# Two images side by side in a fixed order in one layer, overlapping phases in the next: one change to a four-layer kernel

## The chip, the cores and the metric

The kernel runs on one core of a Trainium2 chip. The core has five engines that work side by side, each with its own in-order queue: TensorE (PE, matrix products into PSUM), VectorE (DVE, element-wise work), ScalarE (ACT, functions by table), GpSimd (POOL), and SyncE (SP), which issues most DMA transfers. The metric is the device time of one execution in microseconds (us). All data is float32.

## The reference

The input is `x`, four images of 128 channels and 64 x 64 pixels. Four layers follow each other:

- Layer 0: self-attention over the 4096 pixels of each image.
- Layer 1: two quantized 3 x 3 convolutions, each followed by an "adder" convolution (a sum of absolute differences) with batch norm, and a residual.
- Layer 2: per image `x = x + attention(norm(x))`, then `x = x + mlp(norm(x))`.
- Layer 3: illumination and gradient maps split the image, then a selective scan along the 4096 pixels.

The change touches layer 2 and the preparation ahead of layer 3's scan. Layer 2 in the reference, cut:

```python
def _biasfree_ln(x, w):              # over the 128 channels of a pixel
    mu = jnp.mean(x, axis=1, keepdims=True)
    var = jnp.mean((x - mu) ** 2, axis=1, keepdims=True)
    return x / jnp.sqrt(var + EPS) * w[None, :, None, None]
...
    x1, x2 = (x[:, :C2], x[:, C2:])                       # 64 + 64 channels
    x1 = _gelu(_conv(x1, dw_w, dw_b, groups=C2, pad=1))   # depthwise 3 x 3
    x2 = _gelu(_conv(x2, qkvl_w, qkvl_b))                 # q, k, v, lfeat, 32 channels each
...
    qk = jnp.einsum('bcn,bdn->bcd', qf, kf)               # of pooled q and k, 32 x 32
...
    return jnp.concatenate([x1, lfeat, out], axis=1)
...
    h = _gelu(_conv(x, fc1_w, fc1_b))                     # 128 -> 512 channels
    h = h + _gelu(_conv(h, pos_w, pos_b, groups=h.shape[1], pad=1))
    return _conv(h, fc2_w, fc2_b)                         # 512 -> 128
```

Layer 3 before its scan: a sigmoid gate and a product with the gradient map (the "split" into a low part and the part `fh`), an RMS norm of `fh` over channels, a projection to 2 x 256 channels, a causal convolution with 4 taps and Silu on the first 256 (`xs`), Silu on the others (`sz`), a projection of `xs` to 40 values per pixel, and from 8 of these `delta = softplus(...)` for 256 channels and `du = delta * xs`.

## The kernel before, in words

The kernel is written with tiles and pools: a program in Python issues instructions, each engine executes its own in a planned order, and semaphores are derived from the tiles that are read and written. A pool gives out buffers in turn, and a tile waits until the one that had its buffer is done with. Where an instruction goes through `keep_in_program_order`, its place in its engine's queue is that of the program text; without it a planner may move it forward or back.

An image lies as 128 partitions (channels) by 4096 columns (pixels); a block is 8 rows of the image, 512 columns, one PSUM bank; an image has 8 blocks. `inner(xp, b, k)` is block `k` of image `b` in the residual stream.

Layer 2 (L603 on) goes through the four images one by one.

- `layernorm` (L634) takes block after block: PE averages over channels (L639), DVE subtracts (L641), ACT squares (L642), PE averages (L644), ACT makes the reciprocal root by Ln and Exp (L82, L83), DVE scales (L647).
- The first norm goes to `hp`, an image with a border of zeros. The first 64 channels go through the depthwise convolution on DVE, nine taps of 64 x 4096 (L670, L672) into `x1`, with Gelu on ACT (L673). The other 64 go through PE and Gelu to `x2` (L660, L663). DVE pools q and k (L678 to L685), PE makes the 32 x 32 product (L690 to L696), ACT its Exp. DVE adds `x1` and a part of `x2` to the stream (L711, L712) and, per block, the attention's result (L715, L719).
- The second norm goes to `m`. Then, in two halves of 32 image rows, four groups of 128 hidden channels each: five products with Gelu into `ht` (L740, L743); a depthwise convolution, for group 0 on PE with diagonal matrices (nine products per block, L753, Gelu L760), for groups 1 to 3 on DVE (nine taps of 128 x 2048, L766 and L768, Gelu L771); the sum with `ht` (L772); and the product back to 128 channels, summed over the groups in four PSUM banks (L776). At the end of a half DVE adds the sums to the stream (L781).
- Buffers: four PSUM banks are shared by all small products, four hold the sums; `ht` and `g` have two buffers each.

`layer3_prepare` (L814 on) takes for each image: the split (L857 to L867: a load `mr` of two map rows, two products into `pm`, Sigmoid on ACT, one product into `pg`, two DVE products, and a store to `low_d`), the norm (L874 to L879), for each of two channel halves the projection into `pre` (L888, L889), the causal convolution with four taps of 128 x 4096 (L891, L893) and Silu (L896), stored to `xs_d`; then the gate Silu (L903, L905) to `sz_d`; then four steps `k2` of 1024 columns: products and copies to `xd` (L916, L919), and for both channel halves the softplus `dv` (L929 to L942: product, bias, Abs, Exp, two DVE operations, Ln, two DVE operations) and on POOL `du` (L945), both stored. Six PSUM banks are shared. `ln_and_exp` (L78) loads ACT's table for Ln and Exp ahead of use.

Neither function pins its order, apart from that table load. What is issued next on an engine is the planner's choice among the instructions of the program text.

Of the kernel before, what the change touches and what calls it, by code (L numbers as in the profile page):

```python
# [1 line left out]

# [6 lines left out]
F32 = mybir.dt.float32  # L9
# [7 lines left out]
P = 128  # L17
B = 4
# [36 lines left out]
def col(ap):  # L55

    return ap.rearrange("(p o) -> p o", o=1)
# [28 lines left out]
def inner(x, b, k):  # L86

    return x[b][:, RB * k : RB * (k + 1), :]
# [513 lines left out]

def layer2(tc, cm, xp, ln1, ln2, dw_w, dw_b, qkvl_w, qkvl_b, fc1_w, fc1_b, pos_w, pos_b, fc2_w, fc2_b):  # L603
    nc = tc.nc
    NCH = 4
    with ExitStack() as ctx:
# [3 lines left out]
        ps = ctx.enter_context(tc.tile_pool(name="l2p", bufs=4, space=PSUM))  # L610
# [8 lines left out]
        ln2_sb = load([1], col(ln2), "ln2")  # L619
        dww = load([TAPS], dw_w, "dww")  # L620
        dwb = load([1], col(dw_b), "dwb")
        qw = load([P], qkvl_w, "qw", P // 2)
# [11 lines left out]
        def layernorm(b, w, out, tag):  # L634
            cm.ln_and_exp(tc)
            for k in range(NB):
                src = inner(xp, b, k)
                pm = ps.tile([P, BK], F32, tag="mm", name=f"pm{tag}{b}_{k}")
                nc.tensor.matmul(pm, cm.mean, src, start=True, stop=True)  # L639
                xc = sb.tile([P, BK], F32, tag="xc", name=f"xc{tag}{b}_{k}")  # L640
                nc.vector.tensor_tensor(rows(xc), src, rows(pm), ALU.subtract)  # L641
                nc.scalar.activation(xc, xc, AF.Square)  # L642
                pv = ps.tile([P, BK], F32, tag="mm", name=f"pv{tag}{b}_{k}")
                nc.tensor.matmul(pv, cm.mean, xc, start=True, stop=True)  # L644
                rs = sb.tile([P, BK], F32, tag="rs", name=f"rs{tag}{b}_{k}")
                cm.rstd(nc, rs, pv)
                nc.vector.scalar_tensor_tensor(out(k), src, w, rows(rs), ALU.mult, ALU.mult)  # L647

        for b in range(B):
            x_all = xp[b]  # L650
            hp = big.tile([P, HP, HP], F32, tag="hp", name=f"hp{b}")
            nc.gpsimd.memset(hp[:, 0:HP:HP - 1, :], 0.0)
            nc.gpsimd.memset(hp[:, 1 : HP - 1, 0:HP:HP - 1], 0.0)
            layernorm(b, ln1_sb, lambda k: hp[:, 1 + RB * k : 1 + RB * (k + 1), 1 : 1 + W], "a")
# [3 lines left out]
            for k in range(NB):  # L658
                pq = ps.tile([P, BK], F32, tag="mm", name=f"pq{b}_{k}")
                nc.tensor.matmul(  # L660
                    pq, qw[64:, :], hp[64:, 1 + RB * k : 1 + RB * (k + 1), 1 : 1 + W], start=True, stop=True
                )
                nc.scalar.activation(x2[:, RB * k : RB * (k + 1), :], rows(pq), AF.Gelu, bias=qb)  # L663

            x1 = big.tile([64, H, W], F32, tag="x1", name=f"x1_{b}")
            for t in range(TAPS):
                y, x = divmod(t, 3)
                v = hp[0:64, y : y + H, x : x + W]
                if t == 0:
                    nc.vector.tensor_scalar(x1, v, dww[0:64, 0:1], None, ALU.mult)  # L670
                else:
                    nc.vector.scalar_tensor_tensor(x1, v, dww[0:64, t : t + 1], x1, ALU.mult, ALU.add)  # L672
            nc.scalar.activation(x1, x1, AF.Gelu, bias=dwb[0:64])  # L673


            cs = big.tile([64, H, W // 2], F32, tag="cs", name=f"cs{b}")
            q, kk = slice(0, 32), slice(32, 64)
            nc.vector.tensor_tensor(cs[q], x2[q, :, 0:W:2], x2[q, :, 1:W:2], ALU.add)  # L678
            nc.vector.tensor_tensor(cs[q, :, 1:], cs[q, :, 1:], x2[q, :, 1 : W - 1 : 2], ALU.add)
            nc.vector.tensor_tensor(cs[kk], x2[kk, :, 0:W:2], x2[kk, :, 1:W:2], ALU.max)  # L680
            pf = big.tile([64, H // 2, W // 2], F32, tag="pf", name=f"pf{b}")
            nc.vector.tensor_tensor(pf[q], cs[q, 0:H:2, :], cs[q, 1:H:2, :], ALU.add)
            nc.vector.tensor_tensor(pf[q, 1:, :], pf[q, 1:, :], cs[q, 1 : H - 1 : 2, :], ALU.add)
            nc.vector.tensor_scalar(pf[q], pf[q], 1.0 / 9.0, None, ALU.mult)
            nc.vector.tensor_tensor(pf[kk], cs[kk, 0:H:2, :], cs[kk, 1:H:2, :], ALU.max)  # L685

            pff = pf.rearrange("p a c -> p (a c)")
            pt = ps.tile([P, 8, 64], F32, tag="mm", name=f"pt{b}")
            for j in range(8):
                nc.tensor.transpose(pt[:, j, :], pff[:, bass.ts(j, P)], cm.ident[0:64, 0:64])  # L690
            qkt = sb.tile([P, 8, 64], F32, tag="qkt", name=f"qkt{b}")
            nc.vector.tensor_copy(qkt, pt)
            pqk = ps.tile([P, 32], F32, tag="mm", name=f"pqk{b}")
            d = slice(96, 128)
            for j in range(8):
                nc.tensor.matmul(  # L696
                    pqk[d, :], qkt[:, j, 32:64], qkt[:, j, 0:32], start=(j == 0), stop=(j == 7)
                )
            mx = sb.tile([P, 2], F32, tag="mx", name=f"mx{b}")
            nc.vector.tensor_reduce(mx[d, 0:1], pqk[d, :], AX.X, ALU.max, negate=True)  # L700
            ex = sb.tile([P, 32], F32, tag="ex", name=f"ex{b}")
            cm.ln_and_exp(tc)
            nc.scalar.activation(ex[d, :], pqk[d, :], AF.Exp, bias=mx[d, 0:1])
            nc.vector.tensor_reduce(mx[d, 1:2], ex[d, :], AX.X, ALU.add)
            ri = sb.tile([P, 1], F32, tag="ri", name=f"ri{b}")
            nc.vector.reciprocal(ri[d], mx[d, 1:2])
            nc.vector.tensor_scalar(ex[d, :], ex[d, :], ri[d], None, ALU.mult)
            st = sb.tile([P, 32], F32, tag="st", name=f"st{b}")
            nc.vector.transpose(st[d, :], ex[d, :])

            nc.vector.tensor_tensor(x_all[0:64], x_all[0:64], x1, ALU.add)  # L711
            nc.vector.tensor_tensor(x_all[64:96], x_all[64:96], x2[64:96], ALU.add)  # L712
            for k in range(NB):
                po = ps.tile([P, BK], F32, tag="mm", name=f"po{b}_{k}")
                nc.tensor.matmul(  # L715
                    po[d, :], st[d, :], x2[d, RB * k : RB * (k + 1), :], start=True, stop=True
                )
                o = inner(xp, b, k)[d]
                nc.vector.tensor_tensor(o, o, rows(po[d, :]), ALU.add)  # L719

            m = big.tile([P, H, W], F32, tag="m", name=f"m{b}")
            layernorm(b, ln2_sb, lambda k: m[:, RB * k : RB * (k + 1), :], "b")

            for half in range(2):
                r0 = half * H // 2
                pf2 = [
                    ps_f.tile([P, BK], F32, tag=f"f{s}", name=f"pf2_{b}_{half}_{s}") for s in range(4)
                ]
                for c in range(NCH):
                    u = f"{b}_{half}_{c}"  # L730

                    ht = sb.tile([P, H // 2 + 2, HP], F32, tag="ht", name=f"ht{u}")
                    nc.gpsimd.memset(ht[:, :, 0:HP:HP - 1], 0.0)
                    edge = 0 if half == 0 else H // 2 + 1
                    nc.gpsimd.memset(ht[:, edge, 1 : 1 + W], 0.0)
                    lo = 1 - half
                    for n in (7, 7, 7, 6, 6):
                        ph = ps.tile([P, BK], F32, tag="mm", name=f"ph{u}_{lo}")
                        src = m[:, r0 - 1 + lo : r0 - 1 + lo + n, :]
                        nc.tensor.matmul(  # L740
                            ph[:, : n * W], f1w[:, bass.ts(c, P)], src, start=True, stop=True
                        )
                        nc.scalar.activation(  # L743
                            ht[:, lo : lo + n, 1 : 1 + W], rows(ph[:, : n * W]), AF.Gelu, bias=f1b[:, c : c + 1]
                        )
                        lo += n
                    g = sb.tile([P, HL], F32, tag="g", name=f"g{u}")
                    if c == 0:
                        for s in range(4):
                            pd = ps.tile([P, BK], F32, tag="mm", name=f"pd{u}_{s}")  # L750
                            for t in range(TAPS):
                                y, x = divmod(t, 3)
                                nc.tensor.matmul(  # L753
                                    pd,
                                    diag[:, t, :],
                                    ht[:, RB * s + y : RB * (s + 1) + y, x : x + W],
                                    start=(t == 0),
                                    stop=(t == TAPS - 1),
                                )
                            nc.scalar.activation(g[:, bass.ts(s, BK)], pd, AF.Gelu, bias=pwb[:, c : c + 1])  # L760
# [688 lines left out]
```

## Time and profile before

| | |
|---|---|
| time before, median of 3 runs | 21609.14 us (21584.60 to 21627.24) |
| the profiled execution | 21531.99 us, span 21530.1 us |
| mean granted clock of PE | 0.959 of full speed |
| PE busy | 19660.2 us, 91% |
| DVE busy | 19088.4 us, 89% |
| ACT busy | 17648.1 us, 82% |
| POOL busy | 7450.4 us, 35% |
| layers 0 and 1, with the residual | 0 to 16816 us |
| layer 2 | 16816 to 18152 us |
| layer 3's preparation | 18152 to about 18890 us |
| layer 3's scan | from there to 21530 us |

The profile is of one execution. Busy time is that in which an engine executed something; it is taken from the records of the trace, times are in us from the first instruction. The slices of the span give the busy share of an engine in each of 40 equal parts, in tenths (9 is 90% or more). A row of a group has a source line, engine, operation, output and inputs with their shapes and the count; after the bar the busy time in all and the mean of one in ns; after the second bar the idle time of the engine before them and what ended it. A row of the waits has the engine and its line, what it waited for, the total, how often and the longest. The profiled execution is 0.36% shorter than the median of the runs.

### The profile page before, as it was taken

What the parts mean: (1) busy time and instruction counts of PE and PEld (TensorE: products, weight loads), DVE (VectorE), ACT (ScalarE), POOL (GpSimd) and SP (SyncE); (2) the same over time, 40 slices, a digit from 0 to 9 for tenths busy, and PEclk for the clock granted to TensorE, in tenths of its full rate; (3) what the DMA queues carried; (4) which work ended last, traced back from release to release, by engine and by line L of the source; (5) the groups of instructions that cost most, each with busy time, mean ns of one, the idle gap of its engine ahead of it and who ended that gap; (6) DMA issues with size and microseconds to landing.
All of it is one profiled execution on the core that took longest, in us unless ns stands there. A gap on an engine that the chain in (4) does not pass through costs nothing.

```text
span 21530.1 us, 322927 instructions
## 1 busy us (share of the span) xinstructions
PE 19660.2 (91%) x139180; PEld 6301.1 (29%) x139180; DVE 19088.4 (89%) x12244; ACT 17648.1 (82%) x9117; POOL 7450.4 (35%) x3822
## 2 busy tenths in 40 slices
PE   9998999999999999999999999999999566779998
PEld 4443222222222222222222222222222122223333
DVE  7886999999999999979999999999999666589998
ACT  5665999999999999979999999999999323566666
POOL 5664222222222222222222222222222000189998
PEclk9999999999999999999999999999999777699999
DMA  0001777777777777767777777777777100289997
GB/s 13 13 5 27 151 153 148 152 154 152 152 152 152 150 149 152 154 132 149 149 149 150 149 148 151 147 149 152 149 154 155 52 0 25 108 230 249 252 253 218
DMA packets 573934, 2959.26 MB, mean 137 GB/s; under 512 B 163981, under 2 KB 164885, under 8 KB 240213
## 3 DMA queue, kind: packets, MB, share of 16 engines
q0 software_dynamic: 294912, 2147.61, 49.8%
q1 hardware_dynamic: 277012, 782.60, 12.8%
q8 instruction: 1089, 17.84, 0.3%
q10 hardware_dynamic: 576, 8.39, 0.1%
q14 instruction: 345, 2.82, 0.0%
HBM read 662.02 MB, written 128.78 MB: 37 GB/s over the span
## 4 chain that ended last, share of the span: by engine, by line
PE 45%; issue 15%; DVE 14%; DMA 13%; ACT 11%; POOL 3%; SPq 0%; POOLq 0%; DVEq 0%; ACTq 0%
PE a1pa L424 16%; PE a2pa L424 13%; ACT aa L455 9%; DMA ma<-ma 9%; PE pe L163 4%; PE pav L206 4%; DVE h L1098 3%; DVE ma L478 3%; DVE da L469 2%; DMA du<-du_d 2%; DVE g L768 1%; PE pd L753 1%; PE mg L1113 1%; POOL dbu L1077 1%; POOL ma L480 1%
## 5 line engine op out<-in xcount | busy, mean ns | idle before, releaser
L480 POOL DMA_DIRECT2D ma<-ma x2048 | 3695.5, 1817 | 10893.4 <-DVE ma L478 7653.1
L455 ACT ACTIVATE aa<-a1pb,a1wn 128x4096 f32<-128x4096 f32 x1920 | 6959.8, 3712 | 412.7 <-PE a1pa L424 269.1
L455 ACT ACTIVATE aa<-a2pb,a2wn 128x4096 f32<-128x4096 f32 x1920 | 6963.3, 3712 | 335.1 <-PE a2pa L424 316.2
L424 PE MATMUL a2pa<-aa,a2pick 128*32 128x512 f32 x30720 | 3624.8, 601 | 82.9 <-ACT aa L455 81.6
L424 PE MATMUL a1pa<-aa,a1pick 128*32 128x512 f32 x30720 | 3608.5, 599 | 84.2 <-ACT aa L455 81.9
L469 DVE TENSOR_SCALAR da<-a2pb,a2wa 128x4096 f32<-128x4096 f32 x1408 | 3269.3, 2348 | 295.7 <-PE a2pa L424 295.5
L469 DVE TENSOR_SCALAR da<-a1pb,a1wa 128x4096 f32<-128x4096 f32 x1408 | 3267.7, 2348 | 252.2 <-PE a1pa L424 252.0
L424 PE MATMUL a1pa<-da,a1pick 128*32 128x512 f32 x22528 | 2684.1, 594 | 15.9 <-DVE da L469 15.9
L424 PE MATMUL a2pa<-da,a2pick 128*32 128x512 f32 x22528 | 2678.4, 593 | 17.9 <-DVE da L469 17.9
L478 DVE TENSOR_SCALAR ma<-a2pb,a2wa 128x2048 f32<-128x2048 f32 x2048 | 2528.9, 1280 | 61.8 <-DMA ma<-ma 61.8
L478 DVE TENSOR_SCALAR ma<-a1pb,a1wa 128x2048 f32<-128x2048 f32 x2048 | 2527.9, 1280 | 58.8 <-DMA ma<-ma 58.7
L1113 PE MATMUL mg<-h,ident 128*128 128x512 f32 x4096 | 1953.2, 614 | 209.4 <-ACT m L1122 173.2
L1098 DVE TENSOR_TENSOR_SCAN h<-da,h,dbu 128x1024 f32<-128x1024 f32 x768 | 1804.2, 2349 | 132.7 <-ACT da L1084 42.2
L424 PEld LDWEIGHTS a2pa<-aa,a2pick 128*32 128x32 f32 x30720 | 984.6, 112 | 2498.3 <-issue 2136.7
L424 PEld LDWEIGHTS a1pa<-aa,a1pick 128*32 128x32 f32 x30720 | 980.8, 111 | 2481.8 <-issue 2121.0
L424 PE MATMUL a2pa<-ma,a2pick 128*32 128x512 f32 x8192 | 1096.5, 608 | 235.0 <-DMA ma<-ma 234.7
L200 POOL TENSOR_TENSOR ssum<-ssum,et 128x512 f32<-128x512 f32 x960 | 1228.7, 1280 | 233.4 <-ACT et L195 166.5
L424 PE MATMUL a1pa<-ma,a1pick 128*32 128x512 f32 x8192 | 1092.4, 606 | 190.6 <-DMA ma<-ma 190.4
L424 PEld LDWEIGHTS a1pa<-da,a1pick 128*32 128x32 f32 x22528 | 715.1, 110 | 1739.3 <-issue 1604.5
L424 PEld LDWEIGHTS a2pa<-da,a2pick 128*32 128x32 f32 x22528 | 713.6, 110 | 1737.2 <-issue 1581.4
L461 DVE SCALAR_TENSOR_TENSOR aa<-a2pb,a2wa,aa 128x4096 f32<-128x4096 f32 x256 | 1147.1, 4481 | 80.3 <-ACT aa L455 80.1
L461 DVE SCALAR_TENSOR_TENSOR aa<-a1pb,a1wa,aa 128x4096 f32<-128x4096 f32 x256 | 1147.0, 4481 | 74.9 <-ACT aa L455 74.8
(294 smaller groups left out, 17912.2 us busy)
## 6 DMA issues: line engine op xcount, KB each, us to landing
ma<-ma POOLq DMA_DIRECT2D x2048, 1024.0 KB, 8.8
dl<-delta_d SPq DMA_DIRECT2D x256, 512.0 KB
dl<-delta_d SPq DMA_DIRECT2D x512, 256.0 KB
du<-du_d SPq DMA_DIRECT2D x256, 512.0 KB
du<-du_d SPq DMA_DIRECT2D x512, 256.0 KB
xs_d<-xs SPq DMA_DIRECT2D x8, 2048.0 KB
sz_d<-sz SPq DMA_DIRECT2D x64, 256.0 KB
delta_d<-dv SPq DMA_DIRECT2D x32, 512.0 KB
```

The lines of the kernel that those rows point to most:

```text
L163: nc.tensor.matmul(pe, k[:, bass.ts(j, P)], unit[u, "q"], start=True, stop=True)
L200: nc.gpsimd.tensor_tensor(unit[u, "sum"], unit[u, "sum"], at, ALU.add)
L206: nc.tensor.matmul(unit[u, "av"], image[u // NB][2][:, j, :], at, start=(j == 0), stop=(j == NJ - 1))
L424: then(nc.tensor.matmul(pa[k][32 * g : 32 * g + 32, :], pick[v][:, 31 - jj : 63 - jj], d[:, bass.ts(4 * at + g, BK)], start=(n // 32, k) n ...
L455: then(nc.scalar.activation(rows(at), view(n, t), AF.Abs, bias=bias, scale=scale))
L461: then(nc.vector.scalar_tensor_tensor(rows(at), view(n, ADDED_TAP), weight(n, ADDED_TAP), rows(at), ALU.max, ALU.add))
L469: then(nc.vector.tensor_scalar(rows(dt), view(n, t), weight(n, t), None, ALU.max))
L478: then(nc.vector.tensor_scalar(rows(mt), v, weight(n, t), None, ALU.max))
L480: then(nc.gpsimd.dma_start(ms[1], ms[0], accum_op=ALU.add))
L753: nc.tensor.matmul(pd, diag[:, t, :], ht[:, RB * s + y : RB * (s + 1) + y, x : x + W], start=(t == 0), stop=(t == TAPS - 1),)
L1098: then(nc.vector.tensor_tensor_scan(t[:, cols][:, s], da[:, s], st[n, "dbu", h][:, cols][:, s], 0.0 if e % 4 == 0 else st["last"], ALU.mul ...
L1113: then(nc.tensor.matmul(pm, cm.ident, st[n, way, h][:, bass.ts(k, BK)], start=(way == 0), stop=(way == 1)))
```

## The change

In layer 2, `first_norm`, `second_norm`, `attention` and `feed_forward` become generators that yield after each step, and a driver steps through two of them in a written order; all their compute instructions go through `keep_in_program_order` (`then`).

- `layernorm` issues in step `s` the mean, subtract and square of block `s`, the second mean, Ln and Exp of block `s - 1`, and the scaling of block `s - 2`.
- The first depthwise convolution reads `hx`, which holds the upper and the lower half of `hp`'s first 64 channels on 128 partitions, brought there by two transfers on SP's queue; a tap is now 128 x 2048.
- The two additions to the stream become transfers from SBUF to SBUF that add (`accum_op`), issued by POOL.
- PSUM: three banks for the small products, one for the attention, four for the sums. `ht` and `g` have three buffers.
- The order: `second_norm(b)` and `first_norm(b + 1)` go beside the last group's taps of image `b - 1`, one tap per two steps; `attention(b + 1)` goes beside `feed_forward(b)`, one step per two. Inside `feed_forward` the products for the next group (`up`) and the dense group of PE (`on_tensor`, three products per step) are issued between DVE's taps (`convolution`).

In layer 3's preparation, `split`, `norm`, `project` and `steps_of` are functions in the same manner. `split(b + 1)` is issued after `project(b)`, and `norm(b + 1)` beside `steps_of(b)`, one step per two. `pre` and the causal convolution go in halves of 2048 columns, the gate in between. The softplus goes in three stages over successive units, with three buffers for `dv`, `ee` and `uu`; `du` is written over `uu`. Eight PSUM banks are shared; `mr` has two buffers in place of three.

```diff
+def together(main, beside, ratio):
+    due = 0.0
+    for _ in main:
+        due += ratio
+        while due >= 1.0:
+            due -= 1.0
+            next(beside, None)
...
-        ps = ctx.enter_context(tc.tile_pool(name="l2p", bufs=4, space=PSUM))
+        ps = ctx.enter_context(tc.tile_pool(name="l2p", bufs=3, space=PSUM))
+        ps_a = ctx.enter_context(tc.tile_pool(name="l2a", bufs=1, space=PSUM))
...
+            hx = big.tile([P, H2 + 2, HP], F32, tag="hx", name=f"hx{b}")
+            for h in range(2):
+                nc.sync.dma_start(hx[64 * h : 64 * h + 64], hp[0:64, H2 * h : H2 * h + H2 + 2, :])
...
-                v = hp[0:64, y : y + H, x : x + W]
+                v = hx[:, y : y + H2, x : x + W]
...
-            nc.vector.tensor_tensor(x_all[0:64], x_all[0:64], x1, ALU.add)
-            nc.vector.tensor_tensor(x_all[64:96], x_all[64:96], x2[64:96], ALU.add)
...
+                then(nc.gpsimd.dma_start(x_all[64:96, half, :], x2[64:96, half, :], accum_op=ALU.add))
...
+                if k == TAPS - 6:
+                    then(nc.scalar.activation(x1, x1, AF.Gelu, bias=dwb))
+                    for h in range(2):
+                        then(nc.gpsimd.dma_start(
+                            x_all[0:64, H2 * h : H2 * h + H2, :], x1[64 * h : 64 * h + 64], accum_op=ALU.add
+                        ))
...
+            yield from up(0, 1)
             for half in range(2):
...
+                after = {0: lambda: gelu(0, 3), 2: lambda: down(0, 3)} if half else {}
+                yield from convolution(half, 1, chain(up(half, 0), up(half, 2)), 1.2, after)
...
+                dense = on_tensor(half)
+                after = {0: lambda: gelu(half, 1), 2: lambda: down(half, 1)}
+                if not half:
+                    yield from convolution(0, 2, chain(islice(dense, 6), up(0, 3)), 1.25, after)
+                    after = {0: lambda: gelu(0, 2), 2: lambda: down(0, 2), 5: lambda: down(0, 0)}
+                    yield from convolution(0, 3, chain(dense, up(1, 1)), 1.25, after)
+                else:
+                    yield from convolution(1, 2, chain(islice(dense, 6), up(1, 3), dense), 1.9, after)
+            gelu(1, 2)
+            yield "last"
+            yield from convolution(1, 3, iter(()), 0, {})
+            yield "rest"
+            down(1, 2)
+            gelu(1, 3)
...
+            tail = until(ended, "rest")
+            together(norms(), tail, 0.5)
+            for _ in tail:
+                pass
+            rest, ended = ended, feed_forward(b)
+            beside = attention(b + 1) if b < B - 1 else iter(())
+            together(chain(rest, until(ended, "last")), beside, 0.5)
+            for _ in beside:
+                pass
...
-        ps = ctx.enter_context(tc.tile_pool(name="l3p", bufs=6, space=PSUM))
+        ps = ctx.enter_context(tc.tile_pool(name="l3p", bufs=8, space=PSUM))
...
-                mr = sb.tile([1, 2, BK], F32, tag="mr", bufs=3, name=f"mr{u}")
+                mr = sb.tile([1, 2, BK], F32, tag="mr", name=f"mr{u}")
...
+        for b in range(B):
+            project(b)
+            if b < B - 1:
+                for _ in split(b + 1):
+                    pass
+            cm.ln_and_exp(tc)
+            beside = norm(b + 1) if b < B - 1 else iter(())
+            for i, _ in enumerate(steps_of(b)):
+                if i % 2:
+                    next(beside, None)
+            for _ in beside:
+                pass
```

## The prediction

> **What bounds the kernel now.** I read the slices of the span first, because the change touches only one stretch of it, then busy time by stage, then the waits inside each stage, and last the duration of one instruction of each group.
>
> ```profile
> PE   9998999999999999999999999999999566779998
> DVE  7886999999999999979999999999999666589998
> PEclk9999999999999999999999999999999777699999
> ```
>
> Nearly all of the span has TensorE (PE) and VectorE (DVE) at nine tenths. Slices 31 to 35 do not: this is layer 2 and the preparation of layer 3. There no engine is full, and TensorE's granted clock is lower. The stages, cut at the first and last instruction of each (columns: length, busy time of PE, its weight loads, DVE, ACT, POOL with counts, then granted clock, DMA share and GB/s):
>
> ```profile
> core 0: us, PE busy (x) PEld busy (x) DVE busy (x) ACT busy (x) POOL busy (x), PEclk, DMA share, GB/s
> 16816.00:18152.00 1336.00, 758.39 (x1626) 309.52 (x1626) 910.86 (x543) 373.99 (x489) 8.81 (x66) 0.77 0.00 1
> 18152.00:18887.00 735.00, 521.71 (x768) 162.24 (x768) 429.61 (x383) 352.34 (x421) 79.22 (x31) 0.67 0.27 105
> 16816.00:16921.00 105.00, 40.81 (x83) 13.11 (x84) 75.69 (x55) 28.95 (x38) 0.48 (x2) 0.61 0.02 6
> 17127.00:17459.00 332.00, 189.53 (x408) 77.36 (x408) 228.32 (x136) 96.61 (x126) 2.44 (x18) 0.77 0.00 0
> 16951.00:16990.00 39.00, 38.52 (x94) 17.38 (x93) 3.04 (x2) 10.71 (x17) 0.24 (x2) 1.00 0.00 0
> 18160.00:18200.00 40.00, 40.00 (x43) 11.66 (x42) 10.68 (x16) 7.35 (x10) 0.00 (x0) 0.50 0.13 47
> ```
>
> Layer 2 takes 1336 us, of which DVE works 911; one steady image takes 332, with DVE 228 and PE 190 in turns. At 16951 PE does dense convolution alone at clock 1.00 while DVE has 3 us of work: a phase where one engine waits for the other. What is waited for (engine, line, releaser, total us, times, longest), layer 2 then layer 3's preparation:
>
> ```profile
> PE pf L776 <- DVE g L772: 242.4, 17, 25.4
> ACT g L771 <- DVE g L768: 211.2, 17, 23.2
> DVE g L772 <- ACT g L760: 200.3, 8, 33.8
> DVE xcb L641 <- PE pmb L639: 73.0, 32, 4.5
> ```
> ```profile
> ACT uu L940 <- DVE ee L939: 108.8, 28, 9.3
> DVE fh L867 <- PE pg L866: 82.2, 29, 5.0
> DVE xd L919 <- PE pxd L916: 65.3, 20, 7.9
> DVE xs L891 <- ACT pre L889: 56.7, 8, 10.0
> ```
>
> DVE is what works most, and it loses 200 us eight times over to PE's dense channel group, and most of the rest to the two norms, one block at a time. The group rows that price the change:
>
> ```profile
> L768 DVE SCALAR_TENSOR_TENSOR g<-ht,pww,g 128x2048 f32<-128x2048 f32 x192 | 444.9, 2348 | 2.9
> L672 DVE SCALAR_TENSOR_TENSOR x<-hp,dww,x 64x4096 f32<-64x4096 f32 x32 | 143.1, 4471 | 0.4
> L711 DVE TENSOR_TENSOR x<-x,x 64x4096 f32<-64x4096 f32 x4 | 17.7, 4417 | 0.1
> L753 PE MATMUL pd<-ht,diag 128*128 128x512 f32 x576 | 249.2, 592 | 0.0
> ```
> ```profile
> L893 DVE SCALAR_TENSOR_TENSOR xs<-pre,cw,xs 128x4096 f32<-128x4096 f32 x24 | 107.6, 4484 | 0.9
> L860 PE MATMUL pm<-mr,iwr 1*128 1x512 f32 x64 | 65.6, 1126 | 0.0
> ```
>
> **Layer 2, DVE work.** The first depthwise convolution goes from 64x4096 to 128x2048. A tap costs by columns, so eight taps at 4.47 and one at 2.34 (38.1 us) become eight at 2.35 and one at 1.28 (20.1): 18.0 saved per image. The adds L711 and L712 (4.42 each, 8.8) become DMAs. DVE's work for an image falls from 228.3 to 228.3 - 18.0 - 8.8 = 201.5. New are two copies from SBUF to SBUF (574 KB each) and four accumulating transfers from POOL. The nearest row is layer 1's accumulating transfer of 1024 KB, 8.8 us to landing and 1.82 us on POOL. Between 0 (landed before the second norm reads) and 4 x (8.8 + 1.8) = 42 us for four images I take 0 where an attention lies beside a feed-forward, since some 20 us of other steps follow the issue, and 9 for image 0, which has nothing beside it. Queued behind them on POOL are only the memsets of `ht`, which a third buffer lets run early.
>
> **Layer 2, PE work.** Per image, at the rates shown in stretches at clock 1.00: 72 dense matmuls at 0.86 (nine in 7.73 us) 62, forty `up` at 0.735 29, 32 `down` at 0.853 27, norms 32 at 0.857 27, attention 20: 166 us. DVE with 201.5 stays the longer one while the mean clock is above 0.82; it is 0.77 now with PE at 57%, and denser work brought it to 1.00 at 16951. I take it that PE, now 70% busy, stays out of the way except where named below.
>
> **Layer 2, how they now lie.** The order is written out, so each stage costs its longer engine plus what the order leaves bare.
> - Start: first norm and attention of image 0, alone, 105 before (16816 to 16921). DVE does 26.8 less and the norm's pipeline may save 10 more (68); the new copies and the last transfer (9 each) in series, with no saving, make 123. Its steps are one chain, so I take 100.
> - Norms beside the nine taps of the previous image's last group: 20 steps. DVE 16 x (0.69 + 0.75) + 20.1 = 43, less pitch overlap 41; a norm block needs 3.4 us from subtract to scale and is spread over three steps of two; with first and last blocks bare, 48. Without taps (image 0) 45.
> - Feed-forward with the next attention: DVE has 201.5 - 41 = 161. Bare are 14 us in the group `convolution(1, 2)`, which carries all twelve dense steps of the half (12 x 2.58 + 4 `up` and 4 `down` and attention = 42 of PE against 28 of DVE), 7 at the turn (`rest`, the first `up`), and 4 of round trips on the attention's single PSUM bank. 186.
> - Image 1 and 2: 48 + 186 = 234 each. Feed-forward 0 lacks a predecessor's rest (three adds and four results, 10) and its turn: 170. Image 3 has one norm, 33, and no attention beside: 6 x 20.1 + 8 x 2.29 + 8 x 0.75 = 145 of DVE, 14 bare, 5 at the end, 197.
> Sum 100 + 45 + 170 + 468 + 197 = 980 against 1336: 356 saved. The ends: if DVE never waits, 4 x 201.5 = 806 (530 saved); if nothing lies beside anything, DVE's saving alone, 4 x 26.8 = 107.
>
> **Layer 3's preparation.** DVE does the same work. The split's three matmuls per block take (65.4 + 65.6 + 61.1) / 32 = 6.0 us, 48 per image, with PE busy 40.00 of 40 us and the clock at 0.50: that bounds the split before and after. Now it runs behind project, whose second half of the convolution (31.6 of DVE per image by L893 and L891) lies beside it. An image 0 to 2: 18 of first half, 58 of split behind ten of gate matmuls, and 80 of softplus steps (DVE 2 x 0.74 + 1.00 + 1.74 + 1.22 + 1.21 + 0.68 = 7.3 per unit, eight units 59, the next norm's 8 x 0.785 beside them, some 15 bare at the turns): 156. Split and norm of image 0 alone 74, image 3 18 + 28 + 74 = 120, less 9 where stages meet: 653 against 739, 86 saved. The activation tables change about three times per image in place of some 13 (17, 13 and 9 loads of 1.28 us stand at L862, L935 and L940); I count this inside the steps, since ACT works 352 of 735 and is not the last. A price I can't read is SP's queue: loads of `mr`, now two buffers, stand between the stores of `sz`, so a store waits for a load that waits for PE's split. Nearest row: ACT waited 41.4 us in all for `sz` stores. I take 0, and 41 for the range's end.
>
> Sum: 356 + 86 = 442. The profiled execution took 21531.99 (span 21530.1), 77 us or 0.36% below the median 21609.14. I take the saving as the same in both: 21090 there, 21167 against the median.
>
> **A rule against it.** The stage of norms at 16816 shows a granted clock of 0.61, PE busy 41 of 105 us. The Trainium skill ("TensorE: Matmul & The Clock Gate", "What's actually happening") says that an idle window of about 3.4 us halves TensorE's rate and one busy window restores it. By this the norms, two matmuls per step, would run cold: an estimate from that page of 2 x 1.71 per step, 68 in place of 48, some 65 us less saved. The same page's second half speaks for more: a busy PE should be at full rate, and the split would take 24 per image, 90 us more saved in all. The row at 18160 contradicts it (busy 40.00 of 40 at 0.50, matmuls with one row of contraction), so the split keeps 48.
>
> **Rivals.**
> - Clock: spread thinly, PE's matmuls keep the clock of 0.67 that layer 3 has. 166 / 0.67 = 248, plus the 33 bare, 281 per image: layer 2 about 1160, 176 saved, with layer 3 21350; half of that effect 21260. For: 0.61 in the norm stage. Against: dense phases ran at 1.00.
> - Layer 3 gains nothing: split, norm, project and steps in series (48 + 21 + 41 + 80 = 190 per image, 760) would lose 21 against 739. Then 21167 + 86 = 21253 to 21275.
> - Better: the bare parts of layer 2 vanish (100 more), and layer 3's steps hide more (50): 21020.
> - Slower: PE never leaves 0.50 in layer 2. One image is then 166 / 0.5 + 33 = 365 against 332, 130 lost over four; with layer 3 in series 20 more: 21760, or with its gain 21653. It decides from 166 / x + 33 = 354 on, a clock of 0.52 (layer 3's gain of 86 then just covers it). Only the split's stretch has such a clock.
>
> **How the numbers follow.** The forecast 0.48, better 0.14, layer 3 without gain 0.16, clock 0.15, slower 0.06, 0.01 no difference. About 0.2% (43 us) is what a measurement of this kernel can tell from no change. All but the last two are faster: 0.93. The range takes the better case at its near end and the clock's: 21030 to 21340. The forecast's own range takes the 42 of transfers and the 41 of SP's queue on one side and half of the bare parts (32 us in each of four images) on the other: 21103 to 21250.
>
> **What would show it.** Right: in layer 2 no wait of DVE for the dense group's Gelu (L760 before) of more than a few us, the first convolution's taps at 128x2048 with 2.35 us, DVE at 85% of layer 2's stretch, images some 234 apart, the split still at 0.50 and about 48. Wrong: a granted clock under 0.7 in layer 2 with PE above 90%; DVE waiting for matmuls of the attention's bank; ACT waiting for `sz` stores longer than 41 us; steps of one image over 95 us.

## The result and the profile after

The changed kernel takes 21224.42 us (median of 4 runs, 21198.92 to 21231.51) against 21600.58 (4 runs) of the kernel before: a ratio of 0.9823 (95% interval 0.9805 to 0.9840), 376 us less. Forecast were 442 less, 21167. Its profiled execution has a span of 21225.8 us, its own time is 21227.61.

To see where the 376 came from I cut both traces at the same instructions: the first scaling of the residual on DVE (L595 before, L596 after), the last result of layer 2 (L781, L867) and the last softplus sum (L942, L1150). The span before the first cut is layers 0 and 1, whose code is the same. The last softplus sum is counted with its usual 1.23 us in both; in the changed kernel its record lasts 3.25, so that by the record itself the preparation is 2 us longer there and the scan 2 shorter.

| stage, us | before | after | less | forecast |
|---|---|---|---|---|
| layers 0 and 1 | 16781.6 | 16845.2 | -63.6 | 0 |
| residual and layer 2 | 1370.9 | 1121.1 | 249.8 | 356 |
| layer 3's preparation | 740.1 | 624.0 | 116.1 | 86 |
| layer 3's scan | 2637.6 | 2635.5 | 2.1 | 0 |

The last three rows give 368, near the timed 376. The first row is no effect of the change: the executions of all kernels in this study, whose layers 0 and 1 are the same, reach the first cut between 16755 and 16860 us. From here on layer 2 and the preparation are compared, which repeat within about 3 us: the same layer 2 came out at 1121.1 and 1120.5 in two programs, the same preparation at 624.0 and 626.8. The scan, the same in all, lay between 2618.8 and 2638.5.

The slices of the span after the change:

```profile
PE   9998999999999999999999999999999777889998
DVE  7886999999999999989999999999999876799998
PEclk9999999999999999999999999999999888799999
```

In slices 31 to 35 PE is fuller than before, DVE in four of the five, and neither is full before the scan begins in slice 35. The stages (layer 2, the preparation, images 2 and 3 of layer 2 from the start of their second norm, counting images from 0, and the first split):

```profile
core 0: us, PE busy (x) PEld busy (x) DVE busy (x) ACT busy (x) POOL busy (x), PEclk, DMA share, GB/s
16880.00:17966.00 1086.00, 774.84 (x1628) 306.39 (x1628) 808.52 (x537) 335.47 (x466) 22.16 (x86) 0.82 0.07 11
17966.00:18590.00 624.00, 496.72 (x768) 157.24 (x768) 426.38 (x426) 292.30 (x384) 79.52 (x31) 0.70 0.32 124
...
17461.40:17734.50 273.10, 194.32 (x410) 76.82 (x409) 200.63 (x132) 83.48 (x117) 5.17 (x20) 0.84 0.07 10
17734.50:17966.00 231.50, 163.08 (x342) 70.48 (x341) 182.93 (x102) 62.54 (x82) 1.98 (x16) 0.82 0.00 0
...
17979.00:18019.00 40.00, 38.99 (x42) 11.16 (x40) 9.46 (x14) 8.14 (x12) 0.00 (x0) 0.50 0.12 47
```

An image's DVE work is 200.6 us, as forecast (201.5). But the image takes 273, not 234: 72 us are bare, not 32. DVE's waits in it:

```profile
DVE x L784 <- PE po L778: 27.9, 5, 13.8
DVE g L845 <- ACT ht L812: 12.4, 1, 12.4
DVE xcb L662 <- PE pmb L660: 11.8, 4, 6.6
DVE g L855 <- ACT g L832: 7.3, 1, 7.3
DVE x L867 <- PE pf L861: 6.4, 1, 6.4
```

The wait for the dense group's Gelu (L855 for L832), 200 us in all before, is 7 in this image now. The waits for the attention's products (L784) and for a first hidden block (L845) were there before in many small pieces, here for the whole of layer 2:

```profile
DVE x L719 <- PE po L715: 36.6, 32, 2.1
DVE g L766 <- ACT ht L743: 12.4, 12, 1.2
```

After the change they are 82.6 and 45.5 us there, and the longest ones 13.8 and 12.4 in place of 2.1 and 1.2. The wait for the norms' means (L662) has become smaller (73.0 before and 29.8 now for the second norm), but in image 2 and at its end it holds single waits of 6.6.

The largest stands in the second half of an image, where one convolution of DVE has all twelve dense steps of PE beside it. First DVE, then PE, in that stretch:

```profile
17682.82 1.28 DVE L845 TENSOR_SCALAR g<-ht,pww 128x2048 f32<-128x2048 f32 x1
17684.15 2.35 DVE L847 SCALAR_TENSOR_TENSOR g<-ht,pww,g 128x2048 f32<-128x2048 f32 x1
17693.88 0.69 DVE L784 TENSOR_TENSOR x<-x,po 32x512 f32<-32x512 f32 x1 [7.39 <-PE po L778]
17694.61 2.35 DVE L847 SCALAR_TENSOR_TENSOR g<-ht,pww,g 128x2048 f32<-128x2048 f32 x1
17696.88 2.29 DVE L855 TENSOR_TENSOR g<-g,ht 128x2048 f32<-128x2048 f32 x1
17699.08 2.35 DVE L847 SCALAR_TENSOR_TENSOR g<-ht,pww,g 128x2048 f32<-128x2048 f32 x1
17715.22 0.69 DVE L784 TENSOR_TENSOR x<-x,po 32x512 f32<-32x512 f32 x1 [13.79 <-PE po L778]
```
```profile
17692.81 1.04 PE L778 MATMUL po<-x,st 32*32 32x512 f32 x2
17699.22 6.51 PE L861 MATMUL pf<-g,f2w 128*128 128x512 f32 x8 [5.38 <-DVE g L855]
17705.56 7.89 PE L826 MATMUL pd<-ht,diag 128*128 128x512 f32 x18
17713.29 0.91 PE L808 MATMUL ph<-m,f1w 128*128 128x448 f32 x2
17714.14 1.04 PE L778 MATMUL po<-x,st 32*32 32x512 f32 x2
```

DVE's small addition (0.69 us) stands at the head of its queue until PE has come through its dense products to the attention's product. That holds back the sum L855, for which PE then idles 5.4 us. In place of one engine bounding, each waits for the other.

The other place is the turn between two images, on PE:

```profile
17514.25 8.57 PE L861 MATMUL pf<-g,f2w 128*128 128x512 f32 x16 [4.93 <-DVE g L855]
17522.75 1.12 PE L705 MATMUL pq<-hp,qw 64*128 64x512 f32 x2
17523.80 3.70 PE L861 MATMUL pf<-g,f2w 128*128 128x512 f32 x8
17527.43 1.12 PE L705 MATMUL pq<-hp,qw 64*128 64x512 f32 x2
17529.33 1.12 PE L705 MATMUL pq<-hp,qw 64*128 64x512 f32 x2 [0.78 <-ACT x L708]
```

PE has idled 4.9 us, and the first eight sums then take 8.57 us. The granted clock is 0.63 in their first 4.0 us (17514.2 to 17518.2) and 1.00 in the 4.6 after that. The Trainium skill ("TensorE: Matmul & The Clock Gate", "What's actually happening") says that an idle window of about 3.4 us halves the rate; this row agrees in kind, for part of those eight. The stop of 5.4 us in the crowded stretch is like it: the four sums behind it take 6.51 us at a granted clock of 0.56. Later in the turn, from 17531.7 to 17538.3, the clock is down to 0.55 again, although no gap of PE in the 9 us ahead is longer than 0.8 us; no run here shows why.

### The profile page after: what moved, and what is told of

Its sections match the earlier page's. It is cut to its first block, busy times and chain, and to the rows that moved or that the text cites. A ratio compares the mean times of both kernels' runs of the same rounds, so it can differ in the third digit from the quotient of the medians.

```text
span 21225.8 us, 322990 instructions
## 1 busy us (share of the span) xinstructions
PE 19655.4 (93%) x139180; PEld 6297.5 (30%) x139180; DVE 18983.7 (89%) x12276; ACT 17548.6 (83%) x9055; POOL 7551.0 (36%) x3838
## 4 chain that ended last, share of the span: by engine, by line
PE 44%; issue 15%; DVE 13%; DMA 13%; ACT 10%; POOL 3%; SPq 0%; DVEq 0%; POOLq 0%; ACTq 0%
PE a1pa L425 15%; PE a2pa L425 13%; DMA ma<-ma 10%; ACT aa L456 9%; PE pe L164 4%; PE pav L207 4%; DVE h L1339 4%; DVE ma L479 3%; DVE da L470 2%; DVE g L847 1%; DMA du<-du_d 1%; POOL ma L481 1%; PE mg L1354 1%; POOL dbu L1318 1%; PE a1pc L375 1%
## 5 line engine op out<-in xcount | busy, mean ns | idle before, releaser
L481 POOL DMA_DIRECT2D ma<-ma x2048 | 3778.3, 1859 | 10882.1 <-DVE ma L479 7604.2
```

The costliest lines, as they stand in the source:

```text
L481: then(nc.gpsimd.dma_start(ms[1], ms[0], accum_op=ALU.add))
```

## The experiments

### One half of the change at a time

```diff
# l2_only: layer3_prepare() as before
# l3_only: layer2() as before
```

> The changed layer 2 with the old preparation of layer 3. In the traces of the two kernels, layer 2 from the first residual operation on DVE to the last result went from 1371 to 1121 us, the preparation from there to the last softplus from 740 to 624, the scan stayed within 2. If the two parts are independent: layer 2 about 1121, the preparation 740, the time 21600 - 250 = 21350. Rival: the two lean on each other (the preparation's start is late or early by what layer 2 leaves on the queues): the preparation differs from 740 by more than 20.

> The old layer 2 with the changed preparation. Independent: layer 2 1371, preparation 624, time 21600 - 116 = 21484. Rival: as for the other half, the preparation differs from 624 by more than 20, because its first split follows another end of layer 2.

Measured: `l2_only` 21325.67 us against 21582.23 of the kernel before (ratio 0.9892, 0.9873 to 0.9910), 257 less; layer 2 1120.5, preparation 737.3. `l3_only` 21462.16 (ratio 0.9949, 0.9934 to 0.9964), 120 less; layer 2 1370.5, preparation 626.8. Together 377, as both at once (376). The halves are independent, so what is missing from the forecast has to be found in layer 2 alone, which lacks 106; layer 3 gives 30 more than forecast.

### The crowded group

```diff
-            together(chain(rest, until(ended, "last")), beside, 0.5)
+            together(chain(rest, until(ended, "last")), beside, 0.55)
```

> One number changed: attention goes on by 0.55 steps per step of the feed-forward in place of 0.5, so its last blocks are issued before the group whose side work is all twelve dense steps. Theory A (in that group DVE stands at the attention's additions, which wait behind dense products on PE, and so issues its sum for the next product late, so that PE idles too): the waits of DVE for the attention's products fall from 14 + 7 us there to under 5, and an image gets about 10 shorter, layer 2 about 1090. Theory B (PE alone bounds that stretch): the wait only moves to the next norm's first block; layer 2 stays at 1121, down by under 10.

Measured: layer 2 1099.4, 21.7 less, between the two theories. The waits of an image (the same image 2):

```profile
DVE xcb L662 <- PE pmb L660: 20.6, 4, 17.1
DVE g L845 <- ACT ht L812: 11.4, 2, 10.4
DVE x L867 <- PE pf L861: 7.2, 1, 7.2
DVE x L784 <- PE po L778: 6.6, 3, 4.8
```

The wait for the attention's products falls from 27.9 to 6.6, and the one for the next norm's mean rises from 11.8 to 20.6. The stretch of image 2 is 13.7 us shorter, that of image 1 8.6, and that of image 0 is 4.1 longer. Both theories hold in part: the mutual wait cost some 12 us in this image, and the rest had been PE's own work, which now shows at the end of the stretch.

```diff
-                yield from convolution(half, 1, chain(up(half, 0), up(half, 2)), 1.2, after)
+                dense = on_tensor(half)
+                early = chain(up(half, 0), up(half, 2), islice(dense, 3 * half))
+                yield from convolution(half, 1, early, 1.2 + 0.3 * half, after)
...
-                    yield from convolution(1, 2, chain(islice(dense, 6), up(1, 3), dense), 1.9, after)
+                    yield from convolution(1, 2, chain(islice(dense, 3), up(1, 3), dense), 1.6, after)
```

> In the second half of an image one of the four dense blocks (three steps, nine products) goes beside the group before. PE has 40 us of products at full clock against 28 of DVE work in the crowded group. Theory B (PE bounds it): 7.7 us off per image and a bit for the attention's blocks that wait less, layer 2 about 1121 - 4 x 9 = 1085. Theory A alone: the waits for the attention's blocks remain, layer 2 shorter by under 15. Theory C (the clock): the moved products run at half rate beside taps, 15 us per image, but hidden there; no difference to B.

Measured: layer 2 1090.8, 30.3 less, close to theory B's 36. Nine products that PE makes elsewhere under DVE's cover are worth 3.5 (the last image, without attention) to 13 us per image.

### The turn, and the single bank

```diff
-            together(chain(rest, until(ended, "last")), beside, 0.5)
+            for _ in chain(rest, islice(ended, 5)):
+                pass
+            together(until(ended, "last"), beside, 0.7)
```

> The attention of the next image starts only after the turn between images (the last sums and the first five products of the new feed-forward), and then goes at 0.7 steps per step, so that it is through before the crowded dense group. At the turn DVE is bare for 6.4 us (for sums on PE, which runs cold at 1.07 us per product) and 12.4 (for the first hidden block). Theory D (the attention's products and Gelus, one after the other through one PSUM bank, stand between): the 12.4 fall to about 5 as in image 0, 7 less for each of three images, and with what 0.55 gave (22) layer 2 about 1075. Rival (the cold clock and the chain of product and Gelu bound the turn): the waits stay near 12, layer 2 about 1099.

Measured: layer 2 1121.6, no gain, worse than both. The turn did get shorter (the wait for the first hidden block 12.4 to 4.4), and the stretches of images 1 and 2 fell by 3.8 and 9.8 us, less than the 8.6 and 13.7 of the 0.55 steps. But the attention, now more tightly packed, waits for its own Gelus (7 to 9 us per image at L718), and the next norm's first mean is 18.8 late. Image 0, which has no turn before it, got 17.0 longer by this, and that took back the gain.

```diff
-        ps = ctx.enter_context(tc.tile_pool(name="l2p", bufs=3, space=PSUM))
-        ps_a = ctx.enter_context(tc.tile_pool(name="l2a", bufs=1, space=PSUM))
+        ps = ctx.enter_context(tc.tile_pool(name="l2p", bufs=4, space=PSUM))
...
-                pq = ps_a.tile([P, BK], F32, tag="at", name=f"pq{b}_{k}")
+                pq = ps.tile([P, BK], F32, tag="mm", name=f"pq{b}_{k}")
# and pt, pqk, po likewise
```

> The attention's products take their PSUM banks from the four that all small products share, in place of one bank of their own and three for the others. Theory G (the single bank's round trip holds the attention and at the turn the feed-forward up): the turn's 12.4 fall by half, image 0's Gelus (21 us bare for eight) by 5, layer 2 about 1095. Rival: a bank is waited for elsewhere instead and the order of products is fixed anyway; layer 2 within 10 of 1121.

Measured: layer 2 1080.9, 40.2 less, more than theory G expected. Of it 16 lie in image 0, whose attention stands alone (from the first cut to the second norm 129.5 us before this edit, 113.5 with it), and 12 and 10 in the stretches of images 1 and 2, where the next attention runs beside. Image 2:

```profile
DVE xcb L661 <- PE pmb L659: 18.4, 5, 6.6
DVE x L783 <- PE po L777: 17.9, 2, 12.7
DVE g L844 <- ACT ht L811: 9.6, 2, 8.1
```

The waits for the attention's products fall from 27.9 to 17.9 and those for the first hidden block from 12.4 to 9.6; the next norm's rise. In image 0 the norm ahead stays as it was (13.6 and 13.9 us), but the attention's first eight products and their Gelus take 8 us in place of 23, and PE's waits for those Gelus fall from 17.3 us to 1.4. A bank of its own for the attention made each of its products wait until the one before had been read, on a queue where others stand behind it. The edit also gives the other small products a share in a fourth bank; in images 1 and 2 the two are not separated.

### Is DVE still what bounds the rest?

```diff
+                    then(nc.vector.scalar_tensor_tensor(x1, v, zero, x1, ALU.mult, ALU.add))
# after each of the eight adding taps; zero is a column of zeros
```

> Each of the eight adding taps of the attention's depthwise convolution is followed by one more that adds zero times the same data: 8 x 2.27 = 18.2 us of DVE work per image more, about what the change took away by going to 128 partitions. Theory F (DVE bounds the feed-forward outside the crowded group and the turn): nearly all of it is paid, 4 x 18 = 73, layer 2 about 1190. Rival (PE bounds layer 2 as a whole by now): only image 0's attention, which lies alone, pays, 18 to 30, layer 2 about 1145.

Measured: layer 2 1177.2, 56 longer for 73 us of added work: 14 in the start, 18, 11 and 14 in the three stretches with an attention beside. DVE bounds most of what lies outside the two bad places. If taking work away gains what adding it costs, the part of the change that halved the taps was worth about that: some 56 of its 72. That is argued from this run and not measured by itself.

### The clock in layer 3's split

```diff
-        iwr = cp.tile([1, P], F32, name="iwr")
-        nc.vector.tensor_scalar(iwr, cm.ones[0:1, :], iwl, None, ALU.mult)
+        iwr = cp.tile([P, P], F32, name="iwr")
+        nc.gpsimd.memset(iwr, 0.0)
+        nc.vector.tensor_scalar(iwr[0:1, :], cm.ones[0:1, :], iwl, None, ALU.mult)
...
+        mrs = [cp.tile([P, 2, BK], F32, name=f"mr{i}") for i in range(2)]
+        for t in mrs:
+            nc.gpsimd.memset(t, 0.0)
...
-                mr = sb.tile([1, 2, BK], F32, tag="mr", name=f"mr{u}")
-                nc.sync.dma_start(mr, maps_d[:, b, c].rearrange("(o i) n -> o i n", o=1))
+                mr = mrs[k % 2]
+                nc.sync.dma_start(mr[0:1], maps_d[:, b, c].rearrange("(o i) n -> o i n", o=1))
```

> In layer 3's split the two products with one row of contraction per block (the map row times a row of weights) are made with 128 rows, 127 of them zeros in data and weights. The result is the same, and each product has the same number of columns. In both traces these stretches have PE busy all the time at a granted clock of 0.50, after some 6 us at full rate when they follow dense work. Theory E (the clock goes by how much of the array is used, not by being busy): the clock rises to 1.00, a block takes 2.6 to 3 us in place of 5.71, the first split 25 in place of 46, the three others 41 to about 25: the preparation goes from 624 to about 555. Rival (the clock here has another cause, or zeros don't count as use): the split stays at 0.50, the preparation at 624.

Measured: the preparation 565.8, 58 less. The second split of the changed kernel, then the first one of this kernel, on PE:

```profile
18056.88 1.02 PE L1028 MATMUL pm<-x,iwm 128*128 128x512 f32 x2
18057.83 1.12 PE L1029 MATMUL pm<-mr,iwr 1*128 1x512 f32 x2
18058.79 1.02 PE L1031 MATMUL pg<-mr,alr 1*128 1x512 f32 x2
...
18063.50 2.08 PE L1028 MATMUL pm<-x,iwm 128*128 128x512 f32 x2
18065.50 2.07 PE L1029 MATMUL pm<-mr,iwr 1*128 1x512 f32 x2
18067.37 1.91 PE L1031 MATMUL pg<-mr,alr 1*128 1x512 f32 x2
```
```profile
17918.57 1.91 PE L1036 MATMUL pg<-mr,alr 128*128 128x512 f32 x2
17920.28 1.49 PE L1033 MATMUL pm<-x,iwm 128*128 128x512 f32 x2
17921.60 1.02 PE L1034 MATMUL pm<-mr,iwr 128*128 128x512 f32 x2
17922.46 1.02 PE L1036 MATMUL pg<-mr,alr 128*128 128x512 f32 x2
```
```profile
17922.00:17938.00 16.00, 16.00 (x39) 7.12 (x38) 8.10 (x12) 4.12 (x6) 0.00 (x0) 1.00 0.27 101
```

With one row of contraction in two of three products, full rate lasts 6.6 us after the dense work ahead and then falls to half, with no idle gap above 0.65 us. The product with 128 rows (L1028) slows down with the other two, from 1.02 to 2.08. With 128 rows in all three the clock rises to 1.00 and stays, though 127 of the rows hold zeros. A steady block takes 2.58 us in place of 5.71, and PE's four splits together 114 us in place of 168. The page's rule that a busy window restores the rate is contradicted by the changed kernel's split (38.99 of 40 us busy at 0.50); what counts as busy depends on how many rows are used. That explains why the forecast, which took the row and not the rule, had the split right.

```diff
+        xdp = [cp.tile([P, 2 * BK], F32, name=f"xdp{i}") for i in range(2)]   # zeros
...
-                        pd, dtw[:, bass.ts(mc, P)], xds[k2][0:DT_RANK, bass.ts(s, BK)], start=True, stop=True
+                        pd, dtw[:, bass.ts(mc, P)], xds[k2][:, bass.ts(s, BK)], start=True, stop=True
```

> On top of the split with 128 rows (preparation 566 us), the low-rank products of the softplus steps, 8 rows of contraction before, are made with 128 rows, zeros in data and weights. Theory E (the clock goes by the used part of the array): in the steps, granted clock 0.6 to 0.7 now, it rises above 0.8, the waits of DVE for those products and the ones behind them (29 + 7 us) halve, the preparation goes to about 545. Rival (in the steps PE idles too often for the clock to rise, and DVE's chain bounds them): clock and preparation stay, 566.

This is on top of the split with 128 rows. Measured: the granted clock of the steps does rise (0.73 to 0.80 over the first image's steps, 0.59 to 0.74 in the 40 us from 28 us after their start, 0.78 to 0.84 over the preparation), the preparation is 563.6 against 565.8. So the mechanism holds a second time and is worth nothing beyond the 3 us within which the stage repeats. Of the rival the half on time holds (PE is not what bounds the steps), the half on the clock does not.

### Together

`both_spread` has the spread dense block, the shared banks, the split with 128 rows, and

```diff
-                sg = sb.tile([P, BK], F32, tag="sg", name=f"sg{u}")
+                sg = sb.tile([P, BK], F32, tag="sg", bufs=3, name=f"sg{u}")
# the same for sz
```

> Three edits that were tried alone, together: one dense block moved out of the crowded group (1121 to 1091 alone), the attention's products in the shared four banks (1081 alone), the split with 128 rows (624 to 566 alone); and the stores of the split and of the gate get three buffers in place of two (waits for them 50 + 37 us on ACT). If the crowded group and the bank are separate costs: layer 2 1121 - 30 - 40 = 1051; if the bank's cost was mostly paid in the crowded group, about 1070. Preparation 566 if ACT's waits are hidden, 545 if not.

Measured: layer 2 1057.8, preparation 556.1. Of the 70 us of the two edits alone 63 add up; the third buffer gives 10 more in the preparation (565.8 with the padded split alone).

```diff
-            yield from convolution(1, 3, iter(()), 0, {})
+            yield from convolution(1, 3, iter(()), 0, {2: lambda: down(1, 2), 5: lambda: down(1, 0)})
             yield "rest"
-            down(1, 2)
             gelu(1, 3)
             yield
-            down(1, 0)
-            yield
# and 0.55 steps of attention per step in place of 0.5
```

> The same with two more edits in layer 2: 0.55 steps of attention per step, and two of the three sums of the last half go beside the last group's taps and the norms, so that at the turn between images PE has 4 products to make in place of 12. Theory (at the turn DVE waits for 12 sums on a cold PE, 6.5 us per image, and for what comes behind them, 8): 5 to 8 less in each of four images and 5 to 7 for the ratio in three, layer 2 another 35 to 50 shorter than its twin. Rival (the wait goes over to the Gelu of the last group, 2.0 us and a table load, now bare): 10 or less.

Measured: layer 2 1090.6, 33 longer than its twin. Image 2:

```profile
DVE xcb L661 <- PE pmb L659: 32.2, 7, 11.0
DVE g L844 <- ACT ht L811: 11.6, 2, 9.0
DVE xca L661 <- PE pma L659: 8.0, 2, 7.7
```

The sums did leave the turn (the wait L866 for L860 falls from 7.3 in the twin to 2.9), but among the norms their eight products stand ahead of the means that DVE needs next: 40 us of waits there, 19 in the twin. Two edits were made at once, so which of them cost how much is not separated.

The first of the two, in five runs:

> The combination of the spread dense block, the shared banks and the split with 128 rows again, timed against the kernel before. Its stages in the look before: layer 2 1058, preparation 556, against 1371 and 740 in the kernel before: 497 less, a ratio of 0.977 to the time before, against 0.9823 of the changed kernel. Rival: stages read in one execution don't add up to a timed difference, for instance because the scan gives some back: under 450 less.

Measured: 21127.46 us (5 runs, 21112.18 to 21144.96) against 21621.63, ratio 0.9772 (0.9759 to 0.9785), 494 less; layer 2 1058.8, preparation 556.1. It beats both kernels. The same program took 21006.9 in its single run as `both_spread`: the first cut came at 16755.2 there and at 16859.8 in the profiled execution here, and the two stages agree within 1 us. These 105 us lie ahead of the changed code, so single times say little here and the stages are compared.

## Why the prediction was right or wrong

- **Direction and range: right.** 21224 lies within 21030 to 21340, and within the forecast's own 21103 to 21250. 376 of the 442 came. The total is nearer than its parts, and that is luck: layer 3's 30 too many cover a part of the 106 that layer 2 lacks.
- **DVE's work per image: right.** 201.5 forecast, 200.6 measured; the taps run at 2.35 us, the two large adds are gone. The transfers that took their place, priced between 0 and 42 us, landed 4.4 and 8.5 us after their issue, and no wait in layer 2 names them.
- **The start and image 0: right.** 100 + 45 + 170 = 315 from the start of layer 2 to the second norm of image 1. Measured from the first cut, 346.5, of which the residual's 34.4 (16781.6 to 16816 before) do not belong to layer 2: 312. Its parts fit too: 95 for the start and 217 for the norm and image 0.
- **The step that failed: what the order leaves bare in images 1 to 3.** The prediction put it at "14 us in the group `convolution(1, 2)`", "7 at the turn" and "4 of round trips on the attention's single PSUM bank". In image 2 the crowded group and the norm behind it leave 31.9 bare (7.4 + 13.8 + 6.6 + 4.1), the turn 18.8 (6.4 + 12.4). The bank, which is part of both, costs 10 to 12 by its own experiment (16 in image 0), and no row stood behind the 4. Another 14 lie in waits that had no term: 7.3 for the dense group's Gelu and 6.7 for the attention's earlier products. Images 1 to 3 took 270, 273 and 232 for 234, 234 and 197: 110 us, all that layer 2 lacks. The place and the engine were named, the sizes were not: I had counted the products of PE against DVE's work as two sums that overlap, and not that both engines stop for each other inside the stretch, nor that PE ran at 0.56 and 0.63 of its clock behind the two stops of 5.4 and 4.9 us. Image 3 has no attention beside it and lacks 35 all the same: there DVE waited 10.8 us for the dense group's Gelu and 15.7 for first hidden blocks.
- **PE's clock: right.** 0.84 in an image against the 0.82 where PE was to become the longer engine. The rival with 0.67 did not occur. The page's cold norms did not either: the norms of image 1 beside taps took 47 us (17191.7 to 17238.6) for 48 forecast and not 68, at a granted clock of 0.91.
- **Layer 3: right in kind, 30 too little.** An image takes 150.6 us (18097.8 to 18248.4, from one image's steps to the next; the next one 153.4) for 156, the split is at 0.50. Split and norm of image 0 took 63 us (17966 to 18029) where I had 74. SP's queue, which I took at 0, added nothing: ACT waited 41.6 us for the gate's stores, 41.4 before. A third buffer showed that the waits for the two kinds of stores were worth 10, once the split ran at full clock.
- **The rivals.** None occurred. "Better" (21020) needed the bare parts gone: with them partly mended, and the split at full clock, 21127 was reached.
- **The signs: mixed.** The taps at 2.35 us and the split at 0.50 (41 to 46 us per image for some 48) came as said. DVE was to be busy for 85% of layer 2 and images 234 apart; it was 74% (808.5 of 1086.0) and 270 and 273. And one of the signs of being wrong did show: DVE waited 82.6 us in all for the products in the attention's bank.

## What to carry to other kernels

When two pieces of work are interleaved in a fixed order, a stretch doesn't cost the longer of its two sums: count which instruction stands at the head of each queue, since a small addition that waits for a product at the end of PE's queue stops both engines. Give interleaved work no single-buffered link in its chain (40 us here), and spread the other engine's work until no stretch has more of it than cover. And where TensorE is at half clock while busy, look at how many rows its products use.

## What the runs showed of the hardware

A stream in which two of three products have one row of contraction holds the granted clock at 0.50 with PE busy 38.99 of 40 us, and brought it down from 1.00 in 6.6 us. The same products padded with zeros to 128 rows bring it to 1.00, and 5.71 us of three products become 2.58. Eight rows act in the same way (0.73 to 0.80 over one image's steps when padded). Behind idle gaps of 4.9 and 5.4 us PE ran at 0.63 for 4.0 us and at 0.56 for 6.5. Transfers from SBUF to SBUF that add landed 4.4 us (256 KB) and 8.5 us (512 KB) after their issue, beside computing engines. Layers 0 and 1, the same in every program here, differ by up to 105 us between executions (16755 to 16860 to the first cut, both ends with one and the same program), while layer 2 and the preparation repeat within about 3; whether the first cut varies by the transfers there was not tried.
